# Attention masks of layer 1: from engine work to a casting DMA and a transposing DMA

## The chip, the cores and the metric

The kernel runs on one NeuronCore of a Trainium2 chip. The time is device microseconds of one execution of the whole program; the medians below are over three runs. The core has a matrix engine (PE; PEld is its weight load), a vector engine (DVE), a scalar engine (ACT), a general engine (POOL) and a queue for DMAs (SP). POOL can issue DMAs too. Each engine works through its own instructions in a fixed order and waits for the others through semaphores.

## The reference, cut to what matters

There are 32 graphs (batches) of 512 nodes with 256 features. Two layers follow each other; each is a graph step and a feed-forward step. The change touches the graph step of the second layer alone: an attention with 4 heads in which a node attends only to the nodes that `node_adj` (int32, here 0 or 1) connects it with.

```python
def _L1_gnn_ref(nodes_embed, node_adj, W, a_src, a_dst, bias, ln_gamma, ln_beta):
    h = jnp.einsum('bnd,hde->bhne', nodes_embed, W)
    ...
    weight = jax.nn.leaky_relu(weight, negative_slope=0.01)
    weight = jnp.where(node_adj[:, None] == 0, NEG, weight)
    attention = jax.nn.softmax(weight, axis=-1)
    dst = jnp.einsum('bhij,bhje->bhie', attention, h) + bias[None, :, None, :]
    out = jax.nn.relu(dst) + h
```

```python
x = x + _L1_gnn_ref(_layernorm(x, axis=-1), adj, ...)
x = x + _L1_ffn_ref(_layernorm(x, axis=-1), ...)
```

## The kernel before

The first layer (`layer0_sorted`) takes the span up to about 2375 us; the second (`layer1_plain`) begins its constants inside the first one's tail and takes the rest. A general form of both layers stands at the end of the program and runs only if a flag that the fast forms collect in `over` is not zero; it does not run here.

In `layer1_plain` two streams of Python generators are woven together, and the framework's scheduler then fixes the order of the instructions on each engine:

- `attentions()` runs `attention(b)` woven with `prepare(b + 1)`.
- `mixer(g)` runs the feed-forward step of two batches (a pair) and hands out credits, by which the attention stream moves on. `STEPS` is the number of yields that `prepare` is expected to make and goes into `PACE`.

`prepare(b)` gathers the rows of `x` (POOL, L1154, four indirect DMAs), normalizes them (statistics on DVE L1126, a power on POOL L31, the scaling on ACT L1133), turns them (PE L1142), multiplies by `wa` (PE L1180), adds the bias (POOL L1189), and writes a row of 4 x 512 numbers to DRAM (`ownd`, SP L1197) that four DMAs spread over the 128 partitions (`own`, SP L1200). `attention(b)` forms 16 tiles `att` of 128x512 on DVE (L1213: the larger of `own` and `other`, times the mask) and multiplies them on PE (L1249, L1254). `mixer` follows with `lgp` (PE L1335), `sw` (ACT L1336, DVE L1337 to L1342), `yTp` (PE L1347), a scan, `oTp` (L1535), `vp` (L1557), `outp` (L1567), and stores the result (SP L1570).

The mask is the transposed adjacency. The function `masks(b)` makes it, for each of 4 row tiles: SP loads 128x512 int32 (L1079); ACT writes a bf16 copy and its sum of rows (L1093), and the squares with their sum (L1094), from which the last lines of the program check that the entries are 0 or 1 and that no row is empty; PE turns four 128x128 blocks (L1084) into a PSUM bank of the tag "any" (four banks, shared with `lgp`, `yTp`, `hp` and nearly all else); DVE copies them as uint8 into the mask (L1085). Two masks are held at a time. `masks(0)` runs in the tail of the first layer, the others inside `prepare(b)`, whose yields they share.

Of the kernel before, what the change touches and what calls it, by code (L numbers as in the profile page):

```python
# [10 lines left out]
I32 = mybir.dt.int32  # L11
BF16 = mybir.dt.bfloat16
U32 = mybir.dt.uint32
AF = mybir.ActivationFunctionType
ALU = mybir.AluOpType
# [4 lines left out]
P = 128  # L20
N = 512
D = 256
NT = N // P
# [841 lines left out]
def layer1_plain(tc, ident, eps, x2s, ranks, adj, w, out, over, ps):  # L865
# [3 lines left out]
    nc = tc.nc  # L869
    B = adj.shape[0]  # L870
    SEG = B // len(x2s)
    GB = 2
    AH, _, HO = w["W"].shape
# [13 lines left out]
    HE = HO + 1  # L887
    AP = AH // 2
    TURNS = AP * NT + 6
    STEPS = 15  # L890
    WANTED = 68
    AHEAD = 3
    ATT = 2 * (AHEAD + 2) + AP + 1
# [7 lines left out]
    with ExitStack() as ctx:  # L901
# [3 lines left out]
        def ctile(name, shape):  # L905
            return cst.tile(shape, F32, tag=name, name=name)
# [8 lines left out]

        ones = ctile("ones", [P, P])
        nc.gpsimd.memset(ones, 1.0)
        identb = cst.tile([P, P], BF16, tag="identb", name="identb")
        nc.vector.tensor_copy(identb, ident)

        wa = ctile("wa", [P, DC, AH * HO + 2 * AH])
        for c in range(DC):
# [17 lines left out]
                                 start=c == 0, stop=c == DC - 1)  # L940
            nc.vector.tensor_scalar(over[:, : 2 * AH], pn[:, : 2 * AH], SMALL, None, ALU.is_gt)
        yield
        edges = ctile("edges", [P, 2, B * NT])
        abias = const("abias", [P, AH * HO], w["gnn_bias"].rearrange("h e -> (h e)").partition_broadcast(P))
        gamma = const("gamma", [P, AH * HO], w["ln_gamma"].rearrange("h e -> (h e)").partition_broadcast(P))
        beta = const("beta", [P, AH * HO], w["ln_beta"].rearrange("h e -> (h e)").partition_broadcast(P))
# [121 lines left out]
            nc.scalar.activation(ebsl, ebsl, AF.Exp)  # L1068

        se = ctx.enter_context(tc.tile_pool(name="e1", bufs=2, side="right", reuse_waits="tile"))  # L1070
        masked = {}

        def masks(b, bank="any"):

            a, raw = [], []

            def load(t):
                raw.append(se.tile([P, N], I32, tag="ai", name=f"ai{b}_{t}", bufs=2))
                nc.sync.dma_start(raw[t], adj[b, t * P : (t + 1) * P, :])  # L1079

            def turn(t):
                pt = ps.tile([P, NT, P], BF16, tag=bank, name=f"maskp{b}_{t}")
                for j in range(NT):
                    nc.tensor.transpose(pt[:, j, :], a[t][:, j * P : (j + 1) * P], identb)  # L1084
                nc.vector.tensor_copy(mask[:, :, t * P : (t + 1) * P], pt)  # L1085

            load(0)
            load(1)
            yield
            for t in range(NT):  # L1090
                n = b * NT + t
                a.append(se.tile([P, N], BF16, tag="a", name=f"a{b}_{t}", bufs=3))
                nc.scalar.activation(a[t], raw[t], AF.Identity, accum_out=edges[:, 0, n : n + 1])  # L1093
                nc.scalar.activation(raw[t], raw[t], AF.Square, accum_out=edges[:, 1, n : n + 1])  # L1094
                if t + 2 < NT:
                    load(t + 2)
                if t == 1:
                    mask = se.tile([P, NT, N], mybir.dt.uint8, tag="mask", name=f"mask{b}")
                    yield
                if t > 1:  # L1100
                    turn(t - 2)
                    yield
            for t in range(NT - 2, NT):
                turn(t)
                yield
            masked[b] = mask

        yield from masks(0, "mm")
        yield True
        ps = ctx.enter_context(tc.tile_pool(name="p1", bufs=4, space=PSUM, reuse_waits="tile"))  # L1110
        sb = ctx.enter_context(tc.tile_pool(name="s1", bufs=2, reuse_waits="tile"))
# [9 lines left out]
        def normed(xt, xn, name):  # L1121

            mv = sb.tile([P, NT, 2], F32, tag="mv" + name[0], name=f"mv{name}")
            for t in range(NT):
                st = sb.tile([P, 6], F32, tag="st" + name[0], name=f"st{name}_{t}", bufs=4)
                nc.vector.bn_stats(st, xt[:, t, :])  # L1126
                nc.vector.bn_aggr(mv[:, t, :], st)
            rs = sb.tile([P, NT], F32, tag="rs" + name[0], name=f"rs{name}")
            deviation(nc, rs, mv[:, :, 1], eps)
            shift = sb.tile([P, NT], F32, tag="shift" + name[0], name=f"shift{name}")  # L1130
            nc.vector.scalar_tensor_tensor(shift, mv[:, :, 0], -1.0, rs, ALU.mult, ALU.mult)
            for t in range(NT):
                nc.scalar.activation(xn[:, t, :], xt[:, t, :], AF.Identity, bias=shift[:, t : t + 1],  # L1133
                                     scale=rs[:, t : t + 1])
# [13 lines left out]
        def prepare(b):  # L1148

            while b >= AHEAD_X and b - AHEAD_X not in stored:  # L1150
                yield True
            xt = xs[b] = sb.tile([P, NT, D], F32, tag="x", name=f"x{b}", bufs=AHEAD_X)
            for t in range(NT):
                nc.gpsimd.indirect_dma_start(  # L1154
                    out=xt[:, t, :], out_offset=None, in_=x2s[b // SEG],
                    in_offset=bass.IndirectOffsetOnAxis(
                        ap=ranks[:, b * NT + t : b * NT + t + 1].bitcast(U32), axis=0))

            hv = sb.tile([P, NT, AH, HE], F32, tag="hv", name=f"hv{b}")
            xn = hv.rearrange("p t h e -> p (t h e)")[:, : NT * D].rearrange("p (t d) -> p t d", t=NT)  # L1160
            edged = masks(b) if b not in masked else range(3)
            for i, _ in enumerate(edged):
                if i < 3 or b not in masked:
                    yield
                if i == 2:
                    normed(xt, xn, f"c{b}")
                    nc.gpsimd.tensor_add(xt, xt, beta.unsqueeze(1).to_broadcast([P, NT, D]))
                    yield
            mask = masked.pop(b)
            xnT = yield from turned(xn, "x3T", f"x3T{b}")  # L1170
            yield


            ht = sb.tile([P, NT, AH * HO], F32, tag="ht", name=f"ht{b}")
            other = sb.tile([P, NT, AH], F32, tag="other", name=f"other{b}")
            mine = sb.tile([P, AH, NT], F32, tag="mine", name=f"mine{b}")
            for t in range(NT):
                ph = psum("any", f"hp{b}_{t}")
                for c in range(DC):
                    nc.tensor.matmul(ph[:, : AH * (HO + 2)], xnT[:, c, t * P : (t + 1) * P], wa[:, c, :],  # L1180
                                     start=c == 0, stop=c == DC - 1)
                d = ph[:, AH * HO : AH * HO + AH]
                nc.scalar.activation(mine[:, :, t], ph[:, AH * (HO + 1) : AH * (HO + 2)], AF.Exp, scale=1.0 - SLOPE)
                nc.scalar.activation(hv[:, t, :, HO], d, AF.Exp)
                nc.scalar.activation(other[:, t, :], d, AF.Exp, scale=SLOPE - 1.0)
                nc.scalar.copy(ht[:, t, :], ph[:, : AH * HO])
                yield

            nc.gpsimd.tensor_add(hv[:, :, :, :HO], ht.rearrange("p t (h e) -> p t h e", h=AH),  # L1189
                                 abias.rearrange("p (h e) -> p h e", h=AH).unsqueeze(1).to_broadcast([P, NT, AH, HO]))  # L1190
            yield
            pt = psum("any", f"minep{b}")
            nc.tensor.transpose(pt[: AH * NT, :P], mine.rearrange("p h t -> p (h t)"), ident)
            row = sb.tile([AH * NT, P], F32, tag="turned", name=f"turned{b}", bufs=1)
            nc.scalar.copy(row, pt[: AH * NT, :P])
            own_row = dr.tile([AH, N], F32, tag="own", name=f"ownd{b}")
            nc.sync.dma_start(own_row.rearrange("h (t p) -> (h t) p", p=P), row)  # L1197
            own = [wide("own", f"own{b}_{h}", AH + 1) for h in range(AH)]
            for h in range(AH):
                nc.sync.dma_start(own[h], own_row[h].partition_broadcast(P))  # L1200
            for t in range(NT):
                nc.vector.tensor_mul(hv[:, t, :, :HO], hv[:, t, :, :HO], hv[:, t, :, HO:].to_broadcast([P, AH, HO]))
            ready[b] = mask, ht, hv, other, own
            yield
# [11 lines left out]
        def attention(b):  # L1216

            mask, ht, hv, other, own = ready[b]
            xt = xs[b]
# [8 lines left out]
            def back(src, kind):  # L1228

                dst = psum("pv", f"{kind}{b}")  # L1230
                for t in range(NT):
                    nc.tensor.transpose(dst[:, t * P : (t + 1) * P], src[:, t * P : (t + 1) * P], ident)
                return dst
# [32 lines left out]
                nc.scalar.copy(vT[q], pv[q])  # L1266
            yield
            dt = back(dT, "dp")
            rs = sb.tile([P, NT, AH], F32, tag="rs", name=f"rs{b}")
            nc.vector.tensor_scalar_max(rs, dt.rearrange("p (t h e) -> p t h e", t=NT, h=AH)[:, :, :, 0], 1e-30)  # L1270
            nc.vector.reciprocal(rs, rs)
# [326 lines left out]


        flags = over[:, 2 * AH + 3 :]  # L1600
        nc.vector.tensor_sub(flags, edges[:, 1, :], edges[:, 0, :])
        nc.vector.tensor_scalar(flags, flags, 0.0, None, ALU.not_equal)
        nc.vector.tensor_scalar(edges[:, 0, :], edges[:, 0, :], 0.5, None, ALU.is_lt)
        nc.vector.tensor_add(flags, flags, edges[:, 0, :])


def layer1(tc, ident, eps, x2, adj, w, out):
# [632 lines left out]
```

## Time and profile before

| | us |
|---|---|
| median of 3 runs (4462.54 to 4462.93) | 4462.75 |
| the profiled execution, its own time | 4459.08 |
| its span, first to last instruction | 4456.4 |
| span of the window 2412 to 4300, second layer in its steady part | 1888 |
| start of `x4T10p` to start of `x4T12p` (one pair of batches) | 3091.3 to 3217.6 |

The profile is one execution. "Busy" is the time in which an engine had an instruction in work; the groups give a count, a mean duration, and the idle time just before them with what ended it. The timeline lists instructions in order of time, with the idle time before them in brackets.

### The profile page before, as it was taken

The numbers are of one execution on the slowest core, as the hardware profiler recorded it, in microseconds if no ns is written. First come the engines' busy times: TensorE is split into PE (matmuls) and PEld (weight loads), VectorE is DVE, ScalarE is ACT, GpSimd is POOL, SyncE is SP. The second block draws the span as 40 slices with busy tenths as digits, with TensorE's granted clock in tenths as the row PEclk, the third lists the DMA queues.
The fourth block names the chain that finished last, engine by engine and source line by source line (L and its number), as shares of the span: only waits on it lengthen the run. The fifth ranks groups of instructions, "written<-read, shape, count | busy, mean of one in ns | idle before, by whom it ended". The sixth has DMA issues, their size and how long they took to land.

```text
span 4456.4 us, 57911 instructions
## 1 busy us (share of the span) xinstructions
PE 3922.0 (88%) x20311; PEld 2470.6 (55%) x20311; DVE 3347.2 (75%) x7008; ACT 2291.6 (51%) x4756; POOL 1718.8 (39%) x2036
## 2 busy tenths in 40 slices
PE   5568898899988999888997899999999999999987
PEld 4454565566656656545554455555555555555555
DVE  6668887897788987877766777767677877778763
ACT  3345565566564665556654544544545444454433
POOL 2357644664446644454314232332222232332220
PEclk8679999999999999989998999999999999999998
DMA  5546543664436543564422111111111111111100
GB/s 133 160 144 223 190 130 122 210 200 139 156 117 213 187 147 129 162 201 167 138 81 67 36 53 57 56 48 58 51 43 42 53 55 55 58 48 58 41 15 16
DMA packets 235107, 474.21 MB, mean 106 GB/s; under 512 B 38299, under 2 KB 114075, under 8 KB 234804
## 3 DMA queue, kind: packets, MB, share of 16 engines
q0 software_dynamic: 98688, 315.94, 22.2%
q1 hardware_dynamic: 136116, 154.46, 11.0%
q8 instruction: 162, 2.65, 0.2%
q14 instruction: 141, 1.16, 0.1%
HBM read 413.16 MB, written 57.16 MB: 106 GB/s over the span
## 4 chain that ended last, share of the span: by engine, by line
DVE 34%; PE 32%; DMA 11%; issue 9%; POOL 9%; ACT 5%; SPq 0%; POOLq 0%; DVEq 0%; ACTq 0%
DVE att L1213 5%; DVE acc L637 4%; PE clsp L623 3%; PE avp L1249 3%; PE po L652 3%; PE gatep L623 3%; DMA rows<-table,xs 2%; PE yTp L1347 2%; DVE sw L1337 2%; DVE sw L1342 2%; DVE best L598 2%; DMA rows<-table,tops 2%; DVE sst L1340 2%; DMA best<-table,xs 2%; PE xp L1400 1%
## 5 line engine op out<-in xcount | busy, mean ns | idle before, releaser
L623 PE MATMUL clsp<-xnT,wc 128*128 128x512 f32 x1024 | 520.8, 627 | 49.7 <-ACT cls L625 37.6
L623 PE MATMUL gatep<-xnT,wg 128*128 128x512 f32 x1024 | 499.8, 607 | 10.5 <-ACT gate L625 7.7
L652 PE MATMUL po<-wd,acc 128*128 128x256 f32 x2048 | 455.4, 381 | 6.1 <-DVE acc L641 3.8
L1213 DVE SCALAR_TENSOR_TENSOR att<-own,other,mask 128x512 f32<-128x512 f32 x512 | 392.9, 796 | 79.0 <-DMA own<-ownd 79.0
L652 PEld LDWEIGHTS po<-wd,acc 128*128 128x128 f32 x2048 | 388.3, 191 | 72.1 <-issue 9.2
L598 DVE SCALAR_TENSOR_TENSOR best<-rows,xs,best 128x1024 f32<-128x1024 f32 x212 | 274.4, 1295 | 121.9 <-ACT best L592 76.4
L637 DVE SCALAR_TENSOR_TENSOR acc<-past,fld,acc 128x512 f32<-128x512 f32 x448 | 345.7, 775 | 24.9 <-ACT past L636 16.9
L632 ACT ACTIVATE acc<-tz,fld 128x512 f32<-128x512 f32 x256 | 198.8, 777 | 269.3 <-PE tz L630 240.1
L623 PEld LDWEIGHTS gatep<-xnT,wg 128*128 128x128 f32 x1024 | 196.0, 196 | 252.3 <-issue 197.9
L636 ACT ACTIVATE past<-tz,fld 128x512 f32<-128x512 f32 x448 | 291.4, 693 | 68.1 <-DVE acc L637 66.6
L1347 PE MATMUL yTp<-sw,x 128*128 128x512 f32 x512 | 264.6, 655 | 64.3 <-DVE sw L1342 59.6
L595 POOL DMA_INDIRECT rows<-table,xs x212 | 249.5, 1177 | 171.6 <-DVE best L598 119.0
L1249 PE MATMUL avp<-att,hv 128*32 128x512 f32 x2048 | 298.9, 607 | 5.6 <-DVE att L1213 5.6
L623 PEld LDWEIGHTS clsp<-xnT,wc 128*128 128x128 f32 x1024 | 181.5, 198 | 188.1 <-issue 111.8
L434 PE MATMUL pm<-h,adj 128*128 128x258 f32 (+1 forms) x1024 | 181.2, 324 | 99.9 <-DVE keep L427 33.7
L1300 POOL TENSOR_TENSOR mu<-mu,eps 128x16 f32<-128x16 f32 x32 | 111.6, 3487 | 391.1 <-DVE mu L1299 391.0
L1335 PE MATMUL lgp<-wsl,x4T 128*128 128x512 f32 x512 | 242.8, 613 | 15.7 <-ACT sw L1336 6.8
L1154 POOL DMA_INDIRECT x<-x2s,ranks x128 | 135.9, 1062 | 298.1 <-DVE att L1213 148.1
L625 ACT ACTIVATE gate<-gatep,fld 128x512 f32<-128x512 f32 x256 | 175.5, 685 | 142.6 <-PE gatep L623 123.8
L553 POOL DMA_INDIRECT xs<-rows_of,order x128 | 156.1, 1219 | 221.5 <-DVE acc L637 100.8
L1567 PE MATMUL outp<-v,swT 128*128 128x256 f32 x1024 | 227.6, 381 | 0.0
L625 ACT ACTIVATE cls<-clsp,fld 128x512 f32<-128x512 f32 x256 | 176.1, 688 | 93.9 <-PE clsp L623 55.6
(599 smaller groups left out, 8978.1 us busy)
## 6 DMA issues: line engine op xcount, KB each, us to landing
adj<-in_adj POOLq DMA_DIRECT2D x128, 256.0 KB
ai<-in_adj SPq DMA_DIRECT2D x128, 256.0 KB
own<-ownd SPq DMA_DIRECT2D x128, 256.0 KB
rows_of<-keep SPq DMA_DIRECT2D x32, 550.0 KB
x<-in_x SPq DMA_DIRECT2D x32, 512.0 KB
x2s<-xs SPq DMA_DIRECT2D x32, 512.0 KB
out<-x SPq DMA_DIRECT2D x32, 512.0 KB
rows<-table,xs POOLq DMA_INDIRECT x212
```

The costliest lines, as they stand in the source:

```text
L595: nc.gpsimd.indirect_dma_start(out=row, out_offset=None, in_=table, in_offset=bass.IndirectOffsetOnAxis(ap=idxs[:, k : k + 1].bitcast(U32) ...
L598: nc.vector.scalar_tensor_tensor(m, row, vals[:, k : k + 1], m, ALU.add, ALU.max)
L623: nc.tensor.matmul(pf, wf[:, c, f * P : (f + 1) * P], xnT[:, c, :], start=c == 0, stop=c == DC - 1)
L625: nc.scalar.activation(o, pf, fn, bias=fld[:, f, bf : bf + 1], scale=1.0 if fn == AF.Gelu else 0.5)
L636: nc.scalar.activation(r, z, AF.Relu, bias=fld[:, f, AT + b : AT + b + 1])
L637: nc.vector.scalar_tensor_tensor(y, r, fld[:, f, CH + b : CH + b + 1], y, ALU.mult, ALU.add)
L652: nc.tensor.matmul(po[:, i, :], acc[f][:, t * P : (t + 1) * P], wd[:, f, :], start=f == 0, stop=f == FC - 1)
L1213: nc.vector.scalar_tensor_tensor(e, own[h], other[:, j, h : h + 1], mask[:, j, :], ALU.max, ALU.mult)
L1249: nc.tensor.matmul(pv[p][k * HW : (k + 1) * HW, :], hv[:, j, h, e : e + HW], weighed[b, h, j], **ends)
L1335: nc.tensor.matmul(pf, xnT[:, c, t * P : (t + 1) * P], wsl[:, c, :], start=c == 0, stop=c == DC - 1)
L1347: nc.tensor.matmul(py, xn[:, t, c * P : (c + 1) * P], sw[:, t, :], start=t == 0, stop=t == NT - 1)
L1567: nc.tensor.matmul(po[:, :D], swT[:, k, t * P : (t + 1) * P], v[:, k, :], start=k == 0, stop=k == KC - 1)
```

## The change

The mask of a batch no longer passes through the engines. `shorten(b)` issues on POOL one DMA that reads the whole adjacency of a batch (512x512 int32, 1 MB) and writes it as bf16 to a tile in DRAM (0.5 MB). `turn(b)` issues on SP one transposing DMA that reads this tile and writes the mask, 128x4x512, now bf16, into SBUF. `keep_in_program_order` ties each casting DMA, for the scheduler, behind the instruction traced last on POOL. Casts 0 and 1 and the first transpose are issued in the tail of the first layer; `prepare(b)` issues transpose `b` and cast `b + 2`.

The checks change too: one ACT instruction per batch takes the squares of (mask - 0.5) over the whole mask and their sum (they are all 0.25 if the entries are 0 or 1); its elementwise result goes to `ht`, which is overwritten later. Empty rows are found by one small DVE instruction on the sums that the attention divides by. `STEPS` goes from 15 to 12, as `prepare` yields three times less, and the bf16 identity goes.

```diff
-    STEPS = 15
+    STEPS = 12
...
-    identb = cst.tile([P, P], BF16, tag="identb", name="identb")
-    nc.vector.tensor_copy(identb, ident)
...
-    edges = ctile("edges", [P, 2, B * NT])
+    edges = ctile("edges", [P, B + B * NT])
+    centre = ctile("centre", [P, 1])
+    nc.gpsimd.memset(centre, -0.5)
...
-        def masks(b, bank="any"):
...
-            def load(t):
-                raw.append(se.tile([P, N], I32, tag="ai", name=f"ai{b}_{t}", bufs=2))
-                nc.sync.dma_start(raw[t], adj[b, t * P : (t + 1) * P, :])
...
-                pt = ps.tile([P, NT, P], BF16, tag=bank, name=f"maskp{b}_{t}")
-                for j in range(NT):
-                    nc.tensor.transpose(pt[:, j, :], a[t][:, j * P : (j + 1) * P], identb)
-                nc.vector.tensor_copy(mask[:, :, t * P : (t + 1) * P], pt)
...
-                nc.scalar.activation(a[t], raw[t], AF.Identity, accum_out=edges[:, 0, n : n + 1])
-                nc.scalar.activation(raw[t], raw[t], AF.Square, accum_out=edges[:, 1, n : n + 1])
...
+        def shorten(b):
+            if b < B:
+                short[b] = dr.tile([N, N], BF16, tag="short", name=f"short{b}", bufs=3)
+                tc.keep_in_program_order(nc.gpsimd.dma_start(short[b], adj[b], max_dma_last_dim=8192))
+        def turn(b):
+            if b < B:
+                masked[b] = se.tile([P, NT, N], BF16, tag="mask", name=f"mask{b}")
+                nc.sync.dma_start_transpose(masked[b], short.pop(b))
+        for b in range(2):
+            shorten(b)
+            yield
+        turn(0)
...
-            edged = masks(b) if b not in masked else range(3)
...
+            if b:
+                turn(b)
+            shorten(b + 2)
+            yield
+            yield
+            yield
+            normed(xt, xn, f"c{b}")
...
+            nc.scalar.activation(ht.rearrange("p t e -> p (t e)").bitcast(BF16), mask.rearrange("p t n -> p (t n)"),
+                                 AF.Square, bias=centre, accum_out=edges[:, b : b + 1])
...
+            nc.vector.tensor_scalar(edges[:, B + b * NT : B + (b + 1) * NT],
+                                    dt.rearrange("p (t e) -> p t e", t=NT)[:, :, 0], 0.0, None, ALU.is_le)
```

More of the change, by code (lines that the diff above doesn't have):

```diff
@@ L1070, in layer1_plain @@
         se = ctx.enter_context(tc.tile_pool(name="e1", bufs=2, side="right", reuse_waits="tile"))
-        masked = {}
-        def masks(b, bank="any"):
-            a, raw = [], []
-            def load(t):
-                raw.append(se.tile([P, N], I32, tag="ai", name=f"ai{b}_{t}", bufs=2))
-                nc.sync.dma_start(raw[t], adj[b, t * P : (t + 1) * P, :])
-            def turn(t):
-                pt = ps.tile([P, NT, P], BF16, tag=bank, name=f"maskp{b}_{t}")
-                for j in range(NT):
[L1084 to L1088, printed above, removed]
-            yield
[L1090 to L1093, printed above, removed]
-                nc.scalar.activation(raw[t], raw[t], AF.Square, accum_out=edges[:, 1, n : n + 1])
[L1095 to L1108, printed above, removed]
+        short, masked = {}, {}
+        def shorten(b):
[8 more added lines that the diff above has]
+            shorten(b)
+            yield
+        turn(0)
         yield True
@@ L1160, in prepare @@
             xn = hv.rearrange("p t h e -> p (t h e)")[:, : NT * D].rearrange("p (t d) -> p t d", t=NT)
-            edged = masks(b) if b not in masked else range(3)
[L1162 to L1168, printed above, removed]
+            if b:
[5 more added lines that the diff above has]
+            normed(xt, xn, f"c{b}")
+            nc.gpsimd.tensor_add(xt, xt, beta.unsqueeze(1).to_broadcast([P, NT, D]))
+            yield
             mask = masked.pop(b)
```

7 lines of the change are left out of this document (3 added, 4 removed).

## The prediction

> **What bounds the kernel now.** I began with the page's busy shares and its chain of work that ended last, then cut out the second layer, since only that is touched.
>
> ```profile
> PE 3922.0 (88%) x20311; PEld 2470.6 (55%) x20311; DVE 3347.2 (75%) x7008; ACT 2291.6 (51%) x4756; POOL 1718.8 (39%) x2036
> ...
> DVE 34%; PE 32%; DMA 11%; issue 9%; POOL 9%; ACT 5%; SPq 0%; POOLq 0%; DVEq 0%; ACTq 0%
> ```
>
> The chain alternates between DVE and PE, so a saving on either may count. The table of windows, for the steady second layer (columns: span; busy time and instruction count of PE, PEld, DVE, ACT, POOL; granted clock, DMA share, GB/s), says which is nearer to full there:
>
> ```profile
> 2412.00:4300.00 1888.00, 1750.18 (x11491) 1035.71 (x11493) 1400.03 (x2983) 918.00 (x2368) 542.70 (x406) 0.98 0.16 50
> ```
>
> PE is busy 1750.18/1888 = 93%, DVE 74%, ACT 49%, POOL 29%. PE's idle time is 138 us, 9.2 per pair of batches (15 pairs of 126 us). What it waited for in that window (total, times, longest):
>
> ```profile
> PE yTp L1347 <- DVE sw L1342: 59.6, 36, 3.0
> PE oTp L1535 <- ACT yT L1529: 13.3, 14, 1.1
> ...
> PE maskp L1084 <- ACT sw L1336: 7.0, 6, 1.3
> ...
> PE maskp L1084 <- DVE mask L1085: 3.3, 4, 1.0
> ```
>
> So a pair has two halves. In the long one (scan, attention products, `oTp` to `outp`) PE works back to back. In the short one, where `sw` is normalized, PE ends up waiting 59.6/15 = 4.0 us per pair for DVE. DVE's own timeline there shows the mask in that chain:
>
> ```profile
> 3226.71 0.16 DVE L1131 SCALAR_TENSOR_TENSOR shiftc<-mvc,rsc 128x4 f32<-128x4 f32 x1 [1.22 <-POOL rsc L31]
> 3226.79 0.68 DVE L1085 CAST mask<-maskp 128x512 uint8<-128x512 bf16 x1
> ...
> 3234.59 0.68 DVE L1085 CAST mask<-maskp 128x512 uint8<-128x512 bf16 x1
> ...
> 3237.10 2.62 DVE L1342 TENSOR_TENSOR sw<-sw,sst 128x512 f32<-128x512 f32 x1
> ```
>
> From 3226.71 to the last `sw` at 3239.7 DVE has no gap, and two mask casts lie inside. PE's timeline ends the same stretch with `yTp` at 3239.77 after 2.58 idle, released by that `sw`.
>
> **What goes away.** The groups give the whole amounts:
>
> ```profile
> L1085 DVE CAST mask<-maskp 128x512 uint8<-128x512 bf16 x128 | 85.9, 676 | 1.2 <-PE maskp L1084 0.8
> L1084 PE MATMUL maskp<-identb,a 128*128 128x128 bf16 x512 | 45.5, 221 | 11.5 <-ACT sw L1336 7.0 <-DVE mask L1085 3.3 <-ACT a L1093 1.2
> L1093 ACT ACTIVATE a<-ai 128x512 bf16<-128x512 int32 x128 | 80.6, 630 | 93.8 <-PE outp L1567 54.5 <-PE maskp L1084 15.5 <-PE bp L1232 13.6
> ```
>
> A. PE transposes. Starts are closer than durations: four take from 3217.41 to the next matmul at 3217.63, 0.22 us; at 3299.28 eight hold PE for 0.54. So 4 x 0.22 = 0.9 us per batch. One batch's set lies in the back-to-back half: 15 x 0.9 = 13.5 us, counted. The other set (3217, 3221, 3227, 3231) lies ahead of the `yTp` wait; PE would only wait longer there, so 0, bound 13.5.
>
> B. The two casts in the gapless DVE stretch, 0.60 us each by the next start (3226.79 to 3227.39, 3234.59 to 3235.19): 1.2 x 15 = 18 us, off the `yTp` wait. Bounds 0 and all 59.6.
>
> C. Waits for the PSUM bank or the cast (`maskp` 3.3, and 7.0 behind `sw`): they too lie ahead of the `yTp` wait; 0, bound 10.3.
>
> D. The other casts. The one at 3309.09 holds up `mix`, 0.61 us, but PE waited for `mix` only twice, 2.1 us in all, because attention products fill it. 0, bound 0.61 x 15 = 9.
>
> E. The eight ACT instructions per batch (0.63 and 0.2 us each, 213 us over the kernel): ACT is at 49% and 93.8 us of its idle time stands ahead of `a` alone. 0. The start of the layer is another matter:
>
> ```profile
> 2375.00:2416.00 41.00, 16.08 (x64) 11.94 (x65) 21.42 (x60) 14.57 (x52) 27.49 (x30) 0.63 0.34 103
> ...
> 2408.74 1.97 PE L1142 MATMUL x3T1p<-ident,hv 128*128 128x128 f32 x8 [9.97 <-DVE mask L1085]
> ```
>
> PE is busy 39% of that time and `x3T1p` waits 9.97 us for a bank that a mask holds. That wait goes. But POOL, busy 27.5 of 41 us, now gets five casting DMAs (batches 2 to 6) before the first bias addition L1189. At one `adj` row each (575 ns, below) that is 2.9 us, at four rows 11.5. Net 5 us gained; bounds 10 gained, 8 lost.
>
> **What is added, in order of queue.** By the compiled orders, cast `b + 2` stands on POOL right behind the four gathers of `x(b)`, and ahead of `rsc` (L30, L31) in even batches and of `mu` (L1300) in odd ones. It waits for DMA lanes only. No casting DRAM-to-DRAM copy is in the trace; the nearest rows are
>
> ```profile
> L392 POOL DMA_DIRECT2D adj<-in_adj x128 | 71.6, 575 | 16.1 <-DVE own_part L169 9.7 <-issue 5.1
> ...
> 3224.47 1.08 POOL L30 TENSOR_TENSOR rsc<-mvc,eps 128x4 f32<-128x4 f32 x1 [4.31 <-DVE mvc L1127]
> ```
>
> Issue: between one such row, 0.575, and four (1 MB against 256 KB), 2.3 us, plus the 0.30 that stands between gathers. I take 0.9, the descriptor count (128) being nearest to one row. POOL idles 4.31 before `rsc`, so even 2.6 is covered; uncovered, `rsc` would be late, then `shiftc`, then B's whole stretch: 2.6 x 15 = 39. Before `mu` it idled 2.52 at 3111.20, and none at 3233.50, where DVE used `mu` 4.1 us after its end (3236.83 to `av` at 3240.90). 0 there, bound 15 x 2.6 = 39.
>
> Data of the cast: 1.5 MB at q0's rate (315.94 MB in 0.222 x 4456.4 us = 319 GB/s) is 4.7 us per 63 us on DMA engines 16% busy: 0. In the first layer's tail two casts share the ring with the `rows` gathers, which are on the chain: 3 us lost, bounds 0 and 10 (F).
>
> The transposing DMA: no row of the kind. On data alone 0.5 MB costs 1.7 us at q1's rate (154.46 MB in 0.110 x 4456.4 = 315 GB/s); as 2048 pieces of 256 B at q1's 57.6 ns a packet and engine (0.110 x 4456.4 x 16/136116), 7.4 us. On SP it holds 0.33 us like the plain `ownd` issue, or 0.33 for each of its 128 tiles of 16x128, 42 us. Behind it on SP stand `ownd` and the four `own` of batch b, for which `att` waits; ahead, it waits for the readers of the mask two batches back. Here are these ends:
>
> ```profile
> 3243.84 0.74 DVE L1213 SCALAR_TENSOR_TENSOR att<-own,other,mask 128x512 f32<-128x512 f32 x1
> ...
> 3262.68 0.33 SPq L1197 DMA_DIRECT2D ownd<-turned  x1
> 3264.03 1.75 SPq L1200 DMA_DIRECT2D own<-ownd  x4
> ```
>
> From the last `att` (3244.5) to `ownd` are 18.2 us, in the next batch (3303.27 to 3324.13) 20.9. I take 7.4, being nearest to the row per packet: 0 on the path. At 42 us it is not covered; that is a rival.
>
> A page of the Trainium skill speaks against this part. "VectorE: DVE Perf Modes", section "The three transpose paths", puts a 128x128 bf16 transpose at 390 ns on TensorE and 1309 ns by DMA; the trace has 221 ns for the TensorE one. Sixteen blocks one after another would be 20.9 us, an estimate from that page, 2.7 more than the smaller gap; with it all on the path the sum would lose 2.7 x 29 = 78 us. No run here shows the DMA figure yet.
>
> The new ACT instruction is 128x2048 long: 128x512 takes 0.59, 128x1024 takes 1.048 (`ht` L1296), so 2.0, plus 0.2 for the sum. In odd batches it stands before `xpad`, where ACT idled 5.90 waiting for PE; in even ones before `mine`, where it idled 7.06 for `yTp`. 0; uncovered, 2.2 x 32 = 70. The small comparison on DVE is like the 0.16 rows and lies beside other DVE work: 0, bound 0.16 x 32 = 5. `att` now reads a bf16 mask in place of uint8; no row has that. The cast alone (0.60 by the next start) and `att` (0.66 by the next start, 0.74 long) are the ends for 128x512 elements, so at most 0.06 x 512 = 31 us of DVE either way, some 10 of it in the short half; I take 0, since the output and two inputs stay as they are.
>
> **Sum.** -13.5 (A) - 18 (B) - 5 (E) + 3 (F) = -33.5. The profiled execution took 4459.08 us, 3.67 under the median and 2.7 over its span; 4459.08 - 33.5 = 4425.6, and on the median 4429. Its own range: with B halved and the start at its lost 8 instead of its gained 5, 9 + 13 less gained, 4451; A, C and D in full besides, 33 more gained, 4396.
>
> **Rivals.** R1, the transposing DMA blocks SP, slower: at 42 us instead of 18.2, `own` comes 24 us late per batch. For it: 128 tiles and no row to show they are issued as one; against: every SP row is 0.33 to 0.38. DVE already waits 79.0 us for `own`, 15 times, so nothing covers it: 24 x 29 = 690, about 5120. It decides from 18 us on; at 23 us it costs 5 x 29 = 140. Chance 0.10.
>
> R2, POOL holds the cast much longer, slower: from 4.31 us on, `rsc` and `mu` are late. At 6 us, 1.7 x 15 + 3 x 15 = 70 against the 33 gained: 4500. For it: POOL's gathers of 128 rows take 0.95, as much as a whole `adj` issue, so the kind of DMA matters; against: the 575 ns row. Chance 0.12.
>
> R3, the gain is bigger: DVE's relief also pulls the other waits, B up to 59.6 and C, D, A in full: 33.5 + 41.6 + 33 = 108 gained, 4355. For it: DVE loses 85.9 us of work; against: PE at 93%. I give the upper part, below 4396, 0.12.
>
> R4, the short half is held by the gathers (`rsc` released by POOL at 3226.71 after 1.22 idle) and the long one by DVE: only a few us of A are kept, or the start loses what they give: 4454 to 4472, chance 0.10. That the casts drift elsewhere is ruled out by the compiled orders.
>
> **Chances.** Forecast 0.56. With 0.2% (9 us) as what a measurement can tell from no change: faster 0.56 + 0.12 = 0.68, same 0.10, slower 0.22. Range 4370 to 4500: below lie half of R3, above R1 and half of R2, 0.06 + 0.16.
>
> **What the profile after would show.** Right: no `maskp`; `yTp`'s wait for `sw` near 42 us in the window; a pair near 124 us; the POOL cast near 0.9 us; the transpose landing within 10 us of its start and `ownd` not held; `x3T1p` without its wait. Wrong: a long SP row ahead of `ownd`, `att`'s wait for `own` well over 79.0, POOL busy across `rsc`, or ACT's square ahead of a copy that PE waits for.

## The result, and the profile after

The changed kernel takes 4490.99 us (median of 4, 4489.6 to 4496.82) against 4462.84 (4462.54 to 4469.04): a ratio of 1.0062, 95% interval 1.0045 to 1.008. It is 28 us slower where 33.5 us faster was forecast. Its profiled execution has a span of 4490.4 us, 34.0 more than before.

The page's busy shares and the chain that ended last:

```profile
PE 3909.7 (87%) x19799; PEld 2452.4 (55%) x19799; DVE 3300.5 (74%) x6909; ACT 2191.8 (49%) x4308; POOL 1743.1 (39%) x2069
...
PE 39%; DVE 28%; DMA 11%; issue 10%; POOL 7%; ACT 5%; SPq 0%; POOLq 0%; DVEq 0%; ACTq 0%
```

Less work and more time. The window of the steady second layer, in the columns used for the kernel before:

```profile
2412.00:4300.00 1888.00, 1704.88 (x10716) 996.69 (x10716) 1334.57 (x2825) 808.21 (x1912) 570.61 (x434) 0.96 0.20 50
```

PE is busy 1705 us of 1888 instead of 1750 and got through fewer instructions: it waits more. The granted clock of PE, the third column from the end, is 0.96 of full speed instead of 0.98; this is taken up below. The waits in that window (PE's, DVE's and POOL's; total, times, longest) say for what:

```profile
PE yTp L1332 <- DVE sw L1327: 100.2, 35, 8.7
PE avp L1232 <- DVE att L1196: 19.9, 4, 10.3
...
DVE av L1288 <- POOL mu L1285: 99.4, 27, 7.7
...
DVE att L1196 <- DMA own<-ownd: 13.4, 21, 2.8
...
POOL x L1134 <- DMA out<-x: 112.1, 16, 16.2
```

PE's wait for `sw` grew from 59.6 to 100.2 us, not to 42. Two waits are new in size: DVE for `mu` on POOL (22.9 before), and POOL's gathers of `x` for the store of `out` (1.8 before). The wait for `own`, the main worry of the forecast, shrank from 79.0 to 13.4; that came with the fewer turns and not with the new masks, since it is 74.6 again in e1 below.

The new instructions themselves cost about what was foreseen. The groups (busy, mean ns; idle before and its releaser):

```profile
L1196 DVE SCALAR_TENSOR_TENSOR att<-own,other,mask 128x512 f32<-128x512 f32 x512 | 367.7, 743 | 13.8 <-DMA own<-ownd 13.4
...
L1156 ACT ACTIVATE ht<-mask,centre 128x2048 bf16<-128x2048 bf16 x32 | 64.1, 2002 | 74.7 <-DVE mu L1283 50.7 <-DMA x2s<-xs 17.5 <-issue 6.5
L1077 POOL DMA_DIRECT2D short<-in_adj x32 | 19.5, 610 | 0.7 <-issue 0.7
```

**Where the 34 us lie.** The first matmul of `x4T0p` starts at 2469.8 us, 10.3 late; the 15 pairs from there to `x4T30p` take 1908.7 us instead of 1886.4, 22.3 more; 1.4 come after. Of the first 10.3, 4.75 are there when the first layer issues its first traced store of `x2s` (429.40 against 424.65), long before a cast at 1969 us; that offset lies between -1.0 and 7.4 us in the runs below, e4 apart, and is no part of the change.

Within the pairs, the starts of PE's groups tell the stage. Means over the pairs 2 to 15, in us, from the timeline (the first start of each group); the last column but one is PE's mean granted clock in the window 2412 to 4300 (which in e4 takes in the end of the first layer):

| kernel | even: `lgp` to `yTp` | even `yTp` to odd `x4T` | odd `yTp` to `rnp` | `yp` to `oTp` | whole pair | PE clock | median, us |
|---|---|---|---|---|---|---|---|
| before | 13.76 | 16.09 | 15.22 | 5.62 | 125.44 | 0.98 | 4462.84 |
| changed | 19.25 | 17.55 | 11.84 | 5.80 | 127.12 | 0.96 | 4490.99 |
| e1, 15 turns | 13.99 | 17.70 | 14.41 | 7.31 | 128.49 | 0.94 | 4502.08 |
| e2, no square | 18.51 | 17.73 | 11.87 | 5.83 | 126.59 | 0.95 | 4482.98 |
| e3, two casts only | 17.21 | 17.67 | 11.81 | 5.85 | 125.58 | 0.96 | 4460.85 |
| e4, casts float | 17.10 | 17.52 | 11.90 | 5.89 | 125.04 | 0.96 | 4535.03 |
| e5, casts late | 17.62 | 17.33 | 14.19 | 5.85 | 127.35 | 0.96 | 4501.86 |
| e9, casts in pairs | 17.81 | 17.72 | 11.91 | 5.85 | 126.40 | 0.96 | 4476.41 |
| e17, `mu` off POOL | 13.98 | 18.26 | 11.84 | 5.64 | 122.49 | 0.97 | 4414.76 |
| e6, six `x` | 13.53 | 16.12 | 11.84 | 5.94 | 120.43 | 0.97 | 4400.13 |
| e11, before, six `x` | 12.22 | 14.65 | 14.84 | 5.82 | 122.55 | 0.98 | 4430.87 |
| e12, its counterpart | 13.22 | 16.24 | 11.86 | 5.92 | 120.07 | 0.97 | 4398.47 |
| e18, six `x`, `mu` off POOL | 12.41 | 15.56 | 11.90 | 5.51 | 117.94 | 0.98 | 4358.06 |

One segment loses 5.5 us a pair: from the first `lgp` of the even batch to its first `yTp`, the stretch in which step B was to gain. The runs of one kernel spread by up to 40 us (4438 to 4478 for the kernel before, over all calls), so a few us are read from this table and not from the medians.

A typical pair shows the chain. POOL of the changed kernel (start, duration, idle before and releaser):

```profile
3613.33 0.61 POOL L1077 DMA_DIRECT2D short<-in_adj  x1
...
3616.72 1.04 POOL L31 TENSOR_TENSOR rsc<-rsc,eps 128x4 f32<-128x4 f32 x1
3621.68 1.07 POOL L1134 DMA_INDIRECT x<-x2s,ranks  x1 [3.92 <-DMA out<-x]
3623.06 0.95 POOL L1134 DMA_INDIRECT x<-x2s,ranks  x1 [0.30 <-issue]
3624.03 2.93 POOL L1285 TENSOR_TENSOR mu<-mu,eps 128x16 f32<-128x16 f32 x1
...
3631.45 2.38 POOL L1148 TENSOR_TENSOR x<-x,beta 128x1024 f32<-128x1024 f32 x1
```

SP of the same kernel there:

```profile
3614.60 0.39 SPq L1555 DMA_DIRECT2D out<-x  x1
```

and its DVE:

```profile
3617.79 0.16 DVE L1111 SCALAR_TENSOR_TENSOR shiftc<-mvc,rsc 128x4 f32<-128x4 f32 x1 [0.33 <-POOL rsc L31]
...
3627.00 1.23 DVE L1288 TENSOR_TENSOR av<-av,mu 128x1024 f32<-128x1024 f32 x1 [7.17 <-POOL mu L1285]
...
3629.94 4.46 DVE L1322 TENSOR_TENSOR sw<-sw,ebsl 128x512 f32<-128x512 f32 x2
```

The store of `out` is issued 1.3 us after a cast. The gather that follows writes the `x` buffer which that store reads, and is let go at 3621.68, 7.1 us after the store's issue. `mu` stands behind two of these gathers on POOL, `av` waits 7.17 us for `mu`, and all of `sw`, which needs none of this, stands behind `av` on DVE; PE's `yTp` follows at 3636.57. In the same pair of the kernel before, `mu` stands behind gathers just as well,

```profile
3606.08 0.95 POOL L1154 DMA_INDIRECT x<-x2s,ranks  x1 [0.30 <-issue]
3607.04 3.17 POOL L1300 TENSOR_TENSOR mu<-mu,eps 128x16 f32<-128x16 f32 x1
```

but DVE's order there puts `av` behind `sw`:

```profile
3604.59 0.16 DVE L1131 SCALAR_TENSOR_TENSOR shiftc<-mvc,rsc 128x4 f32<-128x4 f32 x1 [1.22 <-POOL rsc L31]
...
3607.38 1.30 DVE L1337 TENSOR_TENSOR sw<-sw,ebsl 128x512 f32<-128x512 f32 x2
...
3618.96 1.22 DVE L1303 TENSOR_TENSOR av<-av,mu 128x1024 f32<-128x1024 f32 x1
```

Two things have changed, then: the order on DVE, and the landing of the store. The experiments take them apart.

Two more stand in the rows of the changed kernel, and no experiment was made for them. The two `sw` multiplications at 3629.94 take 4.46 us, where the first two take 1.30 in the kernel before: POOL's addition of `beta` to `x` runs beside them (the kernel before loses 2.1 us that way on a later one; the last section has more). And the long wait lowers PE's clock. PE's timeline, and two stretches in the columns of the window above:

```profile
3636.57 9.62 PE L1332 MATMUL yTp<-sw,x 128*128 128x512 f32 x16 [8.26 <-DVE sw L1327]
```

```profile
3628.80:3636.50 7.70, 0.00 (x0) 0.00 (x0) 7.70 (x10) 0.12 (x1) 4.73 (x4) 0.65 0.49 102
3636.60:3641.20 4.60, 4.60 (x5) 1.62 (x6) 4.60 (x11) 0.00 (x0) 0.00 (x0) 0.50 0.00 0
```

The 16 matmuls of `yTp` take 9.62 us, the first 4.6 of them at a clock of 0.50. In the same pair of the kernel before the clock stays at 1.00, and they take 1.88 and 5.83:

```profile
3613.53 1.88 PE L1347 MATMUL yTp<-sw,x 128*128 128x512 f32 x4
3617.17 5.83 PE L1347 MATMUL yTp<-sw,x 128*128 128x512 f32 x12 [1.76 <-DVE sw L1342]
```

By the clock records of the two traces PE works 4.0 us per pair at 0.5 in the stretch from the even `yTp` to the odd `x4T`, against 1.0 before. Half of the difference, 1.5 us, is an estimate of what this adds there, and the table has 17.55 against 16.09.

### The profile page after: what moved, and what is told of

It reads as the page before. It is cut to its first block, busy times and chain, and to the rows that moved or that the text cites. A ratio compares the mean times of both kernels' runs of the same rounds, so it can differ in the third digit from the quotient of the medians.

```text
span 4490.4 us, 56108 instructions
## 1 busy us (share of the span) xinstructions
PE 3909.7 (87%) x19799; PEld 2452.4 (55%) x19799; DVE 3300.5 (74%) x6909; ACT 2191.8 (49%) x4308; POOL 1743.1 (39%) x2069
## 4 chain that ended last, share of the span: by engine, by line
PE 39%; DVE 28%; DMA 11%; issue 10%; POOL 7%; ACT 5%; SPq 0%; POOLq 0%; DVEq 0%; ACTq 0%
PE yTp L1332 4%; DVE acc L637 4%; PE avp L1232 4%; PE clsp L623 3%; PE gatep L623 3%; PE po L652 3%; DMA rows<-table,xs 3%; DVE att L1196 2%; DVE sw L1322 2%; DVE best L598 2%; PE oTp L1520 2%; PE adp L1237 2%; DMA rows<-table,tops 2%; PE hp L1163 2%; PE outp L1552 2%
## 5 line engine op out<-in xcount | busy, mean ns | idle before, releaser
L1196 DVE SCALAR_TENSOR_TENSOR att<-own,other,mask 128x512 f32<-128x512 f32 x512 | 367.7, 743 | 13.8 <-DMA own<-ownd 13.4
L1332 PE MATMUL yTp<-sw,x 128*128 128x512 f32 x512 | 262.4, 658 | 100.3 <-DVE sw L1327 100.2
L1232 PE MATMUL avp<-att,hv 128*32 128x512 f32 x2048 | 323.1, 604 | 19.9 <-DVE att L1196 19.9
L1134 POOL DMA_INDIRECT x<-x2s,ranks x128 | 150.2, 1173 | 330.8 <-DVE x L1554 118.2
L1332 PEld LDWEIGHTS yTp<-sw,x 128*128 128x128 f32 x512 | 100.3, 209 | 243.3 <-issue 132.4
```

What stands on the lines that cost most here:

```text
L1196: nc.vector.scalar_tensor_tensor(e, own[h], other[:, j, h : h + 1], mask[:, j, :], ALU.max, ALU.mult)
L1232: nc.tensor.matmul(pv[p][k * HW : (k + 1) * HW, :], hv[:, j, h, e : e + HW], weighed[b, h, j], **ends)
L1332: nc.tensor.matmul(py, xn[:, t, c * P : (c + 1) * P], sw[:, t, :], start=t == 0, stop=t == NT - 1)
```

## The experiments

**The first four: turns, square, casts.** e1 puts the three lost turns back, `STEPS` at 15, between the normalizing and the turning of `x`:

```diff
-            yield
+            for _ in range(4 if b else 1):
+                yield
             mask = masked.pop(b)
```

> The changed kernel with the old weave: prepare hands over 15 times again (three more, between the normalizing of x and its turning) and STEPS is 15. Weave theory (the three missing turns shift the attention stream against the mixer, so that the LayerNorm of the attention, av and mu, falls into the stretch of DVE that PE waits for at yTp; wait 100 us there against 59.6): 4425 to 4450, the yTp wait back to 60 or less. Square theory (the new ACT instruction holds up the queue): stays at 4480 to 4495. Cast theory (the casts on POOL and in the ring delay gathers and mu): stays at 4480 to 4495.

Measured 4502.08 (4495.97 to 4515.89), ratio 1.0082 (1.0065 to 1.0099). The segment does return to 13.99 us and `av` to its place behind `sw`, so the order on DVE came with the turns. But the time doesn't: compared with the changed kernel, odd `yTp` to `rnp`, `rnp` onward and `yp` to `oTp` get longer. In the last of these it is the clock again: by e1's records PE works 4.4 us of it at 0.5 (0.3 in the kernel before), behind a wait for `mix` of 2.3 us in the pair at 3605. e15 follows that wait up.

e2 leaves the square out:

> The changed kernel without the ACT square over the mask (the check of the entries is left out). Square theory: 32 x 2.2 us of ACT in front of hp's copies go, 4440 to 4465. Weave theory and cast theory: within 5 us of the changed kernel, 4485 to 4495.

4482.98 (4470.99 to 4491.81), 1.0047 (1.0025 to 1.0069); the segment is 0.74 us shorter, 11 us over 15 pairs. A part of the loss, not most. The square writes `ht`, and so waits for `mu` L1283 (50.7 us in the group above) with the scaling of `hv` behind it on ACT; that this is how it costs is not shown, since the first `sw` multiplications, too, take 115 us in e2's window and not 131.

e3 issues only the first two casts (`if b < 2`), and transposes read these again:

> The changed kernel with only the first two casting DMAs; every later transpose reads one of their two results again (so the masks of batches 2 to 31 are not those of the reference). Cast theory: POOL and the ring are free of 30 casts, DVE's wait for mu falls from 99 us to some 25, 4450 to 4470. Weave theory: only the 0.6 us on POOL twice per pair goes, 4480 to 4491.

4460.85 (4446.78 to 4475.92), 0.9996 (0.998 to 1.0012). Taking 30 casts away gives 30 us, and 2.0 us a pair in that one segment. The same place of a pair, POOL, without them:

```profile
3603.99 1.03 POOL L31 TENSOR_TENSOR rsc<-rsc,eps 128x4 f32<-128x4 f32 x1
3605.22 2.04 POOL L1134 DMA_INDIRECT x<-x2s,ranks  x1 [0.19 <-issue]
...
3608.53 2.93 POOL L1285 TENSOR_TENSOR mu<-mu,eps 128x16 f32<-128x16 f32 x1
```

with the store on SP at

```profile
3601.87 0.39 SPq L1555 DMA_DIRECT2D out<-x  x1
```

The gather starts 3.4 us after the store's issue and doesn't wait for it. The tile's view gives issue to landing of all of them: for `out` without the casts

```profile
DMA to landing us min/median/max: 2.9/2.9/3.3
```

and in e1, which has them, up to 6.7 us:

```profile
DMA to landing us min/median/max: 2.9/3.0/6.7
```

e4 drops `keep_in_program_order`:

> The changed kernel without the order kept for the casts: the scheduler places them. Cast theory: a place that is better or worse by 10 us or more, since the place of the cast matters. Weave theory: within 8 us of the changed kernel, 4483 to 4499, unless the rest of the order moves too.

4535.03 (4527.19 to 4536.59), 1.0157 (1.014 to 1.0174). The scheduler puts all 32 casts at the start of the program, where they keep POOL occupied for 90 us, most of it waiting (the wait is for the casts before):

```profile
42.89 0.52 POOL L1077 DMA_DIRECT2D short<-in_adj  x1 [1.97 <-DMA short<-in_adj]
45.37 0.52 POOL L1077 DMA_DIRECT2D short<-in_adj  x1 [1.97 <-DMA short<-in_adj]
```

The first layer ends 82 us late. The second is then the cheapest of the five-buffer kernels with the changed order, 125.04 us a pair: what e3 found without casts, here with right masks.

**The place of the cast.** e5 moves `shorten(b + 2)` behind the bias addition to `hv`:

> The changed kernel with cast b + 2 issued later in prepare(b), behind the bias addition to hv on POOL instead of behind the gathers of x. The order on DVE stays that of the changed kernel. Store theory (the cast's data, issued 1.3 us before the store of out in the short half, makes the store land after 6.8 us instead of 2.9; the next gathers write the tile that the store reads and wait for it; mu stands behind them on POOL): the wait of the gathers for out falls from 112 us to the 74 us of the run without casts, lgp to yTp of the even batch from 19.3 to 17.2 us, 4455 to 4470. Queue theory (what costs is 0.6 us of POOL for each cast, wherever it stands): 4480 to 4495.

4501.86 (4486.41 to 4511.09), 1.0092 (1.0073 to 1.0112): slower, where the store theory said faster, though the segment did fall to 17.62. The waits of DVE and POOL say what took its place:

```profile
DVE att L1196 <- DMA own<-ownd: 75.7, 27, 4.7
...
POOL x L1134 <- DMA out<-x: 61.8, 5, 16.3
```

The wait for the store fell from 112.1 to 61.8, and the one for `own` rose from 13.4 to 75.7; odd `yTp` to `rnp` lost 2.35 us. Here the casts stand in front of the `own` DMAs and not of the store.

e6 keeps the casts where they were and gives `x` a sixth buffer:

```diff
-            xt = xs[b] = sb.tile([P, NT, D], F32, tag="x", name=f"x{b}", bufs=AHEAD_X)
+            xt = xs[b] = sb.tile([P, NT, D], F32, tag="x", name=f"x{b}", bufs=AHEAD_X + 1)
```

> The changed kernel with six buffers for x instead of five (the generators still hold back as with five; the empty-row flags are written straight into over, to make room), so that a gather writes a tile whose store ended a pair earlier. Store theory: the gathers' wait for out goes altogether, from 112 us to under 10, and the time falls by 25 us or more, to 4440 to 4465. Queue theory: 4480 to 4495, the casts being where they were.

4400.13 (4398.4 to 4413.08), ratio 0.9867 (0.9845 to 0.9889): 91 us under the changed kernel, 63 under the one before. PE's and POOL's waits:

```profile
PE yTp L1332 <- DVE sw L1327: 33.0, 29, 2.3
...
POOL x L1134 <- DMA out<-x: 86.1, 14, 14.7
```

The time came, and more than expected; but the wait by which I meant to see it hardly fell. (Most of both sums is single waits of 14 to 16 us in the other half of a pair, for a store that isn't issued yet.) With a sixth buffer the scheduler issues the gathers a batch earlier, and `shiftc` of both batches goes to the other half, so that the stretch is no longer fed by gathers of its own half. DVE's wait for `mu` on POOL falls from 99.4 to 72.5 us. How much of the 91 us is the store and how much this new order, e6 alone doesn't tell.

e7 joins e1 and e5, e8 joins e5 and e6:

> The first experiment (15 turns, STEPS 15) with the casts issued late as in the fifth. Store theory: the wait there was only 22 us, so little comes back, 4485 to 4505, and the rest of the loss with 15 turns has another cause (DVE's mix of 0.69 us took 2.72 where POOL's addition of outb to x, 2.63 us, ran at the same time). Queue theory: 4495 to 4510.

> Late casts and six buffers for x together. Store theory: no more than one of them gives, since both take away the same wait; 4435 to 4460. If both gains add (4430 or less), the casts also cost by something else than the store.

e7: 4506.21 (4501.84 to 4519.36); e8: 4423.54 (4416.36 to 4429.29), 23 over e6. Late casts lose with six buffers too, the 2.0 us a pair between odd `yTp` and `rnp` being there again (13.88).

e9 issues both casts of a pair behind the second set of gathers (`if b % 2 == 0: shorten(b + 2); shorten(b + 3)`), e10 adds the sixth buffer:

> The changed kernel with both casting DMAs of a pair behind its second set of gathers, so none is in the rings when the store of out is issued. Store theory: lgp to yTp of the even batch from 19.3 to 17.2 to 17.6 us as without casts, and no new wait for own (the collision of the late casts), yTp to rnp of the odd batch stays at 11.8; 4455 to 4470. If it stays at 4485 or more, a cast costs wherever it stands, by what it moves and not by what stands behind it.

> The same with six buffers for x. Store theory: with six buffers the gathers are issued a batch earlier, and the store matters less; 4385 to 4405, at most 15 under the 4400 of six buffers alone. If what the casts cost is the same 22 us in both, 4370 to 4385.

e9: 4476.41 (4466.6 to 4481.68), 1.0022 (1.0004 to 1.0039), the segment at 17.81 and no new wait for `own`. So some 15 us of the casts' 30 are a matter of place; the rest stayed. e10: 4404.81 (4398.27 to 4410.83): with six buffers the place among the gathers no longer matters.

**Is it the change or the buffer?** The kernel before has no room for a sixth buffer; e11 makes it with 12 attention tiles for 13 and 5 `inner` for 6, and e12 gives the changed kernel the same.

> The kernel before with six buffers for x; to make room, the attention tiles have 12 buffers instead of 13 and the inner ones 5 instead of 6. If the sixth buffer alone brings the gain (the kernel before was bound by when the gathers land too), 4395 to 4425. If it needs the work that the change takes off PE and DVE, 4445 to 4475.

> Its counterpart: the changed kernel with six buffers for x and the same 12 and 5. The difference of the two is what the change is worth once the gathers are early: by the prediction's steps A and B 25 to 40 us faster than the kernel before with six; if the loss is still that of the five buffers, none or slower. Beside the 4400 with 13 and 6 it shows what the smaller pools cost: 0 to 15 us.

e11: 4430.87 (4419.7 to 4434.73), 0.993 (0.9908 to 0.9953). e12: 4398.47 (4389.07 to 4405.19), 0.9849 (0.9813 to 0.9885). The buffer alone gives the kernel before some 30 us. And under the same buffers the change is worth 32.4 us between medians whose runs spread by 15 and 16; the forecast's sum was 33.5.

What the buffer does in e11 is not about the store: in the kernel before, the gathers wait 1.8 us for it in all. The groups of `sw`'s two multiplications in the window 2412 to 4300 show what did change (total us; mean ns):

| kernel | `sw<-sw,ebsl` | `sw<-sw,sst` |
|---|---|---|
| before | 100.7; 844 | 91.6; 768 |
| e11, before, six `x` | 80.0; 666 | 82.2; 685 |
| changed | 131.4; 1131 | 84.8; 742 |
| e6, six `x` | 108.5; 880 | 84.5; 686 |

In the kernel before, nearly every pair has one such multiplication of 2.6 to 2.8 us instead of 0.7, beside POOL's addition of `beta` to `x`; the forecast shows one, at 3237.10. In e11 there is none left, and the two groups are 30.1 us shorter, about what e11 gained. In e6 the first group has 251 ns less on each of some 120 instructions, 30 us of the 91. That these groups' time is the run's time is an estimate; no run separates it.

**The order on DVE.** e13 takes the last LayerNorm step a turn later (`i not in (2, 3)`), e16 does it with six buffers, e14 joins e1 and e6:

> The changed kernel, five buffers, but the last step of the attention's LayerNorm is taken a turn later (turns 0, 1 and 4 of the next attention instead of 0, 1 and 3). In the compiled order mu (L1285) then stands on POOL ahead of the second set of gathers, those that wait for the store of out. Chain theory (store, gather, mu, av, sw, yTp, each behind the other on an in-order queue): lgp to yTp of the even batch falls from 19.3 us to 15 or less, 4420 to 4455. If the gathers' landing itself is what the short half waits for: 4475 to 4495 as before.

> The later LayerNorm step with six buffers for x. Chain theory: the two take away the same wait, so little adds, 4385 to 4405. If each takes away a wait of its own, 4370 or less.

> Six buffers for x and the old weave (15 turns). If the weave is what separates the changed kernel from the kernel before, this is the best of all, 4380 to 4400. If the weave of 15 turns only brings DVE's mix under POOL's addition of outb (2 us in each pair, as in the first experiment), 4420 to 4445, above six buffers with 12 turns.

e13: 4593.59 (4585.53 to 4599.14); e16: 4540.16 (4530.69 to 4549.07). The segment fell to 15.26 in e13, but the pair grew to 134.05 us: one turn moves the whole attention against the mixer (10.15 us instead of 3.69 from `x4T` to `lgp`), so nothing can be read from the time. e14: 4449.3 (4435.07 to 4462.23), 49 over e6: with early gathers 12 turns are better than 15.

e17 changes one instruction: DVE's reciprocal stands where POOL's power makes 1/deviation of `mu`'s variance. The LayerNorm then divides by the variance and not by its root, so e17 and e18 do not compute the reference; they serve for the time alone:

```diff
-            nc.gpsimd.tensor_tensor(mu[:, 1, :], mu[:, 1, :], eps[:, 1:2].to_broadcast([P, NG]), ALU.pow)
+            nc.vector.reciprocal(mu[:, 1, :], mu[:, 1, :])
```

> The changed kernel, five buffers, with the power that turns mu into 1/deviation taken off POOL: DVE takes a reciprocal in its place (so the attention's LayerNorm divides by the variance, not by its root). The order on DVE is that of the changed kernel but for this one instruction; the gathers still wait for the store. Chain theory (av and all of sw wait on DVE for mu, and mu on POOL for the gathers): DVE's wait of 99 us for mu is gone, lgp to yTp of the even batch 14 us or less, 4400 to 4445. If the late data of the gathers are what counts: lgp to yTp stays over 17, 4465 or more.

> The same with six buffers for x. Chain theory: the sixth buffer and this one take away the same wait, so together they give little more than each, 4370 to 4400. If they add in full (60 to 90 us under the changed kernel each), 4350 or less.

e17: 4414.76 (4407.14 to 4421.24), 0.9898 (0.9871 to 0.9925), 76 us under the changed kernel with the same five buffers. POOL still waits for the store,

```profile
3590.16 3.87 POOL L1134 DMA_INDIRECT x<-x2s,ranks  x1 [4.03 <-DMA out<-x]
```

but DVE doesn't wait for POOL:

```profile
3588.11 0.24 DVE L1285 RECIPROCAL mu<-mu 128x16 f32<-128x16 f32 x1
...
3588.85 1.22 DVE L1288 TENSOR_TENSOR av<-av,mu 128x1024 f32<-128x1024 f32 x1
...
3591.79 1.28 DVE L1322 TENSOR_TENSOR sw<-sw,ebsl 128x512 f32<-128x512 f32 x2
```

`av` is done before the gather is let go, and the segment is 13.98 us. The late data of the gathers cost nothing there; the queue behind them did. (POOL is also rid of the power's 112 us, so not all of the 76 us need be this wait. The segment gains 5.3 us and the next one loses 0.7, which is 68 over 15 pairs.) e18: 4358.06 (4357.04 to 4361.36), 42 under e6, so the two overlap in part.

**The slow `mix`.** e15 takes e1 and adds `outb` to `x` on DVE instead of POOL:

> The first experiment (15 turns, five buffers) with the addition of outb to x on DVE instead of POOL; DVE gets 32 x 1.2 us more. Collision theory (DVE's 128x512 multiplication of mix by decay takes 2.72 us, not 0.69, while POOL runs its 128x1024 addition): mix goes back to 0.69 us, PE's wait for mix falls from 35 us to under 10, and the time by 10 to 30 us to 4470 to 4492. If mix stays at 2.7 us, the cause is on DVE itself, 4500 or more.

4479.29 (4474.05 to 4484.58), 1.0046 (1.0028 to 1.0064), 23 under e1. The tile view of `mix` in e1 (min, median, max ns; first and last start),

```profile
L1496 DVE TENSOR_TENSOR mix<-mix,decay x14: 2711/2716/2723, 2569.2 to 4241.3; 128x512 f32<-128x512 f32 x14
```

and in e15:

```profile
L1496 DVE TENSOR_TENSOR mix<-mix,decay x14: 681/684/689, 2559.4 to 4206.0; 128x512 f32<-128x512 f32 x14
```

PE's wait for `mix` fell from 35.5 to 21.1 us, less than I said; the time fell as said, to which the clock adds: `yp` to `oTp` has 2.5 us of PE's work at 0.5 instead of 4.4.

## Why the prediction was wrong, point by point

- **The steps that failed.** The miss is 61.5 us, and e3 splits it: 30 go with the casts, and without them the kernel is still 32 above the forecast of 4429.
- **The first: "Data of the cast ... on DMA engines 16% busy: 0."** A mean load says nothing on what the cast stands in front of. The casts cost 30 us (e3), of them about 15 by their place (e9). Likewise "`mu` ... 0 there, bound 15 x 2.6 = 39": it was not the cast's 0.61 us on POOL that made `mu` late, but a gather ahead of `mu`, held by a store whose landing went from 2.9 us without casts (e3) to about 7 behind one. The Trainium skill states what fits this ("DMA: Bandwidth & Descriptors", section "Issuing engines are not separate DMA queues"): transfers started by SP and by GpSimd run on the same 16 DMA engines and interleave. Here the cast is started on POOL and the store on SP.
- **The second: DVE's order in B's stretch, taken as kept.** Right as to place: the stretch from `shiftc` to the last `sw` decides the short half. But I read DVE's order in it from the trace of before. With three turns fewer, `av` moved ahead of `sw` in most pairs (e1 brings it back), and PE's wait grew from 59.6 to 100.2 us. How the 32 us divide is not shown, since e1 has the old order and new losses elsewhere.
- **Two terms that the sum lacked.** It had none for PE's clock, which was 0.98 of full speed in the window and went to 0.96 with the longer waits. And it passed over the `sw` row of 2.62 us at 3237.10, where others take 0.68: POOL's addition runs beside it, and the changed kernel has more of this (1131 ns a multiplication `sw<-sw,ebsl` instead of 844).
- **Step B, 18 us off the `yTp` wait.** The two casts on DVE did go; 5.5 us a pair came in their place. With `mu` off POOL the segment is back at 13.98, with six buffers 13.53.
- **A and the sum.** Under equal, sufficient buffers the change gives 32.4 us (e11, e12) against 33.5. That the totals agree is luck. By the table the two stretches in which B was to gain are 1.00 and 1.59 us longer in e12 than in e11; what is shorter is odd `yTp` to `rnp`, by 2.98, and the rest of the pair, by 2.2, where A was to give 0.9. No run separates the terms further.
- **E and F.** Rather than a gain of 5, the start of the layer lost 2.9 (10.3 at `x4T0p` less 7.4 at the last store of `x2s`), and the first layer from its first such store on lost 2.65 (7.4 less 4.75). Neither is clear of what varies: over the runs the two stretches take 80.5 to 89.1 and 1943.9 to 1957.4 us. The wait of `x3T1p` did go, but PE then stands as long for `att`:

```profile
2404.08 1.92 PE L1122 MATMUL x3T1p<-ident,hv 128*128 128x128 f32 x8
...
2422.42 3.63 PE L1232 MATMUL avp<-att,hv 128*32 128x512 f32 x14 [10.32 <-DVE att L1196]
```

- **The durations.** Cast on POOL 0.61 us (0.9 taken), square 2.00 and 0.19 (2.0 and 0.2), `att` no slower with bf16 (743 ns against 796; in e1, with the same bf16 mask, 802). The square was not free: some 11 us (e2).
- **R1, the transposing DMA.** It holds SP 1.7 to 4.06 us, against the 0.33 or 42 taken, and lands after 4.5, by the view of `mask` in e3:

```profile
DMA to landing us min/median/max: 4.3/4.5/6.4
```

That is under the 7.4 taken; sixteen blocks in 4.5 us are also far from the 20.9 estimated from the page "VectorE: DVE Perf Modes". `own` was not late.
- **R2** came nearest with 4500, by luck: its mechanism, a long hold of POOL by the cast, was not the one (0.61 us), and `rsc` was not late by it.

What stays open: the other half of the casts' cost, which did not go with their place (e9); why e1 loses 2 us from `rnp` to `xp` (8.69 us against 6.73); how the shares of store, order, POOL's addition and clock in e6 divide.

## What to carry to other kernels

When work leaves the engines for the DMA queues, look for the transfer that stands behind it and for what reuses that transfer's buffer: a sixth buffer turned a change from 28 us slower into one 63 us faster than the start, some 30 of it the buffer's own (e11). On an engine that works in a fixed order, ask of each waiting instruction who stands behind it without needing it; here a LayerNorm held up a softmax. When a generator yields less often, compare the compiled orders around the bound before counting instructions. And where one row takes four times what its like take, as `sw` at 3237.10, see which engine runs beside it before adding anything up.

## What the runs showed of the hardware that was not expected

- DVE's 128x512 f32 multiplication takes 2.72 us instead of 0.69 when POOL's 128x1024 f32 addition runs beside it. For `mix` the kernel before avoided it (692 ns on average); for `sw` it did not, see e11. In e1, DVE:

```profile
3602.58 2.72 DVE L1496 TENSOR_TENSOR mix<-mix,decay 128x512 f32<-128x512 f32 x1
```

and POOL:

```profile
3602.11 2.63 POOL L1314 TENSOR_TENSOR x<-x,outb 128x1024 f32<-128x1024 f32 x1 [4.33 <-ACT x L1113]
```

POOL's addition ends at 3604.74, DVE's multiplication 0.56 us later: it began only then, in effect. The `sw` row that the forecast shows at 3237.10 (2.62 us, kernel before) has the same neighbour, which ends at 3239.16, 0.56 us before it:

```profile
3236.83 2.33 POOL L1167 TENSOR_TENSOR x<-x,beta 128x1024 f32<-128x1024 f32 x1
```

This fits the lock that the Trainium skill describes ("SBUF — State Buffer", section "SBUF: two separate sides"): of a DVE instruction with two SBUF inputs and a GpSimd one that reads SBUF, the first to start holds the shared port to its end. With POOL's addition gone, the multiplication takes 0.68 us (e15).

- Casting DMAs of 1 MB int32 to 0.5 MB bf16, DRAM to DRAM, follow each other at 2.48 us (e4), though each holds POOL for only 0.5 to 0.6 us.
- After PE has stood 8.26 us in the pair shown above, the granted clock reads 0.50 until 3641.3 and PE works at it; after 1.76 us in the same pair of the kernel before, it stays at 1.00.
